# A decoder layer on one core: a short path for the last batch, filler matmuls at both ends, and one pair of rows issued by another engine

## The chip, the cores and the metric

The kernel runs on one NeuronCore of a Trainium2 chip. The core has a matrix engine (TensorE, PE in the profile, with its weight loads as PEld), a vector engine (VectorE, DVE), an activation engine (ScalarE, ACT), a general engine (GpSimd, POOL) and an engine that here only starts DMA transfers (SyncE, SP). Each engine runs its own list of instructions strictly in order; semaphores hold it back until what it needs is there. The metric is the device time of one execution in microseconds.

## The reference

32 sequences of 128 tokens by 512 features go through one decoder layer with LayerNorm after each of its three parts:

```python
x = _layernorm(x + _L0_attn_ref(x, Wq, Wk, Wv, Wo))          # causal, 16 heads of 32, rotary
x = _layernorm(x + _L0_xattn_ref(x, ctx, ctx, gamma))
x = _layernorm(x + _L0_ffn_ref(x, w1, b1, ln_g, ln_b, w2, b2))

def _L0_xattn_ref(q, k, v, gamma):       # q, k, v: (32, 128, 512), 8 heads
    qh = q.reshape(B, 8, 16, 512)        # the 512 features are the positions,
    kh = k.reshape(B, 8, 16, 512)        # 16 of the 128 tokens a head
    vh = v.reshape(B, 8, 16, 512)
    sm = softmax(einsum('bhdq,bhdl->bhql', qh, kh) / sqrt(16))
    return gamma * einsum('bhql,bhdl->bhdq', sm, vh).reshape(B, 128, 512)

def _L0_ffn_ref(x, ...):                 # 512 -> 2048 -> 512
    h = gelu(silu(bitlinear158(x, w1, b1)))
    h = layer_norm(h, ln_g, ln_b)
    return bitlinear158(h, w2, b2)       # x: RMS norm, 8-bit steps; w: -1, 0, 1
```

## The kernel before

**Two stages.** Stage one does the self-attention of all 32 batches, splits its result and the context into three bf16 parts, and writes them to HBM (`q_d`, `k_d`; six combinations of parts make one float32-like product). It also makes the FFN's weights ternary. Stage two takes each batch through the cross-attention and the FFN.

**An order written out ahead.** Both stages are lists of operations handed to `Plan` (L83). Each operation has an engine, an estimated cost, what it reads and writes, a priority (batch number plus an offset by kind from `OFF1` or `OFF2`) and sometimes an earliest time `rel`. `Plan.run` (L174) goes through them as a list scheduler: of the operations that could start within the same short interval (`slack`) it takes the one of lowest priority value, and emits its instructions. The result is one fixed order for each engine. The estimated times only make the order; on the chip an engine takes its next instruction when the semaphores let it.

**Start.** `split_weight` (L302) loads Wq and Wk together, Wv and Wo in sixteen tiles of 128x512 into four buffers `wst`. Each is split into a rounded part (`hi`, by ScalarE or VectorE, L315 and L317) and a remainder (`lo`, by VectorE, L318). `load` (L332) brings a batch's x in two forms. A projection (`project`, L346) is twelve matmuls of 128x128x512: hi by hi, lo of x by hi, hi by lo.

**From stage one to stage two.** `split3` (L350) ends a batch of stage one: ScalarE and GpSimd make the three parts, and SyncE issues six writes of them (L364). `early` (L578), run when the last projection is emitted, frees the projection weights' memory and loads K and Q parts of the first two batches of stage two there. In stage two, `b1_` forms for each half batch (four heads) sixteen blocks of scores (L677) of which VectorE takes the row maxima (L681). `shift` (L688) transposes these maxima on TensorE (L691), splits their negative into two bf16 rows (L694, L695), and SyncE copies both rows into the Q tile (L700), so that the second score matmul (`b2_`, L756) subtracts the maximum itself. ScalarE takes the exponential (L759). TensorE multiplies it (L766) with a tile `cT` of 32 columns a head: 16 of V, and 16 of ones, set by GpSimd at L616; so the sum of the weights stands in 16 equal rows beside the 16 result rows. `cT` is one of the tiles of stage two, and its memory held tiles of stage one.

**A batch's end in stage two.** ScalarE copies the result from PSUM to `f` (L773), SyncE writes it to HBM (`F`, L777). `final` (L834) reads back one row of sums a head as a 128x32 tile (`den`), takes the reciprocal (L841), writes it to HBM, reads it broadcast to 128x512 (`rden`), and reads the results as `num`; then num times rden (L846), plus x1 (L848), LayerNorm. `up_` (L896) makes 8-bit steps `q1`, transposes them by DMA (L914), and runs sixteen matmuls (L925) in four blocks, each taken out of PSUM by VectorE (L928). `gelu_` (L934) runs SiLU (L940) and GELU (L942) over the full 2048 columns on ScalarE, each with a table load. `down_` (L946) takes mean and variance (L952, L955), normalizes z (L794, L972 on GpSimd, L980, L991 on VectorE), takes its maximum and square sum (L998, L997), makes steps `q2`, transposes them by DMA (L1003), runs sixteen matmuls (L1009), adds (L1013), LayerNorm, and writes the output (L1016). For the last three batches (`last`) some steps go to VectorE instead of GpSimd and other PSUM banks are used.

The loop at the end of the stage, and the two lines by which shift's rows are copied:

```python
    for b in range(NB2):
        load(b)
        for g in range(2):
            b1_(b, g)
        for g in range(2):
            b2_(b, g)
        final(b)
        up_(b)
...
            for s, m in enumerate((hi, lo)):
                nc.sync.dma_start(q.t[NPR + s:NPR + s + 1].rearrange("p h (a c) -> p (h a) c", c=P), m.t)
```

Of the kernel before, what the change touches and what calls it, by code (L numbers as in the profile page):

```python
# [11 lines left out]
F32 = mybir.dt.float32  # L12
# [11 lines left out]
P = 128  # L24
# [40 lines left out]
CFG = dict(y0e='Pool', x2be='Pool', q2T=1, q1=2, tb2=3, boost=1.0, bank_mT='mx', bank_q1T='m', bank_z='m', bank_q2T='mx', bank_py='m', early=5, ssv=1, NQ=4, cT=3, f=2, num=1, x1=2, rden=2, x2=2, nb=32, mx=3, sT=3, acc=1, m=1, ex=8, mTe='DVE', acce='ACT', q1e='ACT', q2e='ACT', lne='Pool', ye='Pool', sce='Pool', mxw=1, stw=1, pair=1, z=3, xb=3, slack=0.05, last_lne='DVE', last_ye='DVE', last_sce='DVE', last_y0e='DVE', last_bank_mT='sT', last_bank_q1T='m', last_bank_z='sT', last_bank_q2T='mx', last_bank_py='sT', zm='PPPP', last_zm='FFFP', q1m='p', q2m='ad', last_q1m='d', last_q2m='ad')  # L65
OFF2 = {'SP.const': -264.67, 'x.kq': 390.3, 'SP.v': 77.29, 'PE.mx': -381.13, 'DVE.mx': 126.92, 'PE.mT': -632.22, 'DVE.mT': 8.23, 'SP.m': -156.28, 'PE.sT': -531.43, 'ACT.ex': -687.83, 'PE.pv': 37.38, 'ACT.acc': -737.17, 'SP.f': 49.63, 'SP.fd': 1119.71, 'SP.fn': 725.19, 'SP.fx': 343.0, 'DVE.rd': -172.57, 'SP.fr': -316.31, 'SP.fb': 17.98, 'Pool.y': -355.28, 'DVE.y': -82.99, 'Pool.yn': -277.59, 'DVE.c1': -57.25, 'Pool.c1': -358.01, 'Pool.c1m': -627.03, 'Pool.q1a': -78.8, 'Pool.x2b': 72.59, 'SP.q1T': -375.73, 'PE.c1': 39.79, 'DVE.z': -137.9, 'ACT.gelu': -406.78, 'DVE.nmu': -80.22, 'ACT.sq': -333.32, 'Pool.zn': -48.07, 'Pool.zt': 303.63, 'Pool.zb': -221.61, 'ACT.sq2': 252.58, 'DVE.am2': 91.79, 'Pool.c2': -682.87, 'Pool.c2m': -291.19, 'ACT.q2a': -262.61, 'DVE.q2a': -514.12, 'SP.q2T': 382.04, 'PE.c2': 86.97, 'DVE.c3': 17.23, 'Pool.c3': -278.83, 'Pool.c3n': 302.38, 'SP.out': 77.71, 'SP.kq': -42.69, 'DVE.yn': -735.62, 'DVE.c1m': 785.24, 'DVE.q1a': 467.22, 'DVE.zn': 550.15, 'DVE.zb': -508.13, 'DVE.c2m': -306.12, 'DVE.c3n': 99.96}
OFF1 = {'SP.x': 76.47, 'SP.w': -83.56, 'ACT.w': 1251.46, 'DVE.wl': 97.39, 'DVE.w': 1455.82, 'SP.wq': 258.11, 'ACT.wq': -501.07, 'DVE.wq': -718.11, 'PE.wq': 497.75, 'ACT.xh': -83.03, 'Pool.xl': -493.52, 'PE.qkv': 642.06, 'DVE.rope': -749.29, 'Pool.rope': 726.68, 'ACT.v': -277.88, 'SP.cx': 161.38, 'ACT.cs': 561.27, 'Pool.cs': 151.36, 'Pool.cs3': 444.12, 'SP.cs': -169.59, 'SP.ct': -341.75, 'ACT.ct': 5.76, 'SP.cv': 657.35, 'PE.qkT': -233.53, 'DVE.qkT': -713.26, 'PE.sc': 223.31, 'DVE.mask': -673.03, 'ACT.exp': 343.93, 'DVE.rd': 481.16, 'DVE.pr': 893.48, 'PE.prT': -342.18, 'DVE.prT': 602.51, 'ACT.prT': 121.56, 'Pool.pr': 38.32, 'PE.pv': 403.29, 'ACT.oh': 297.53, 'DVE.ol': -241.16, 'PE.wo': 645.28, 'DVE.y': -873.41, 'Pool.y': 255.11, 'Pool.x1': -113.85, 'SP.x1': 730.76, 'ACT.xs': 299.8, 'Pool.xs': -1039.81, 'Pool.xs3': 582.54, 'SP.xs': 975.4}
C1 = dict(pace=15.0, xs=4, pr=5, prT=7, ra=3, qkT=4, sp=3, spr=2, xhe='ACT', lne='Pool', s1e='Pool', s2e='ACT', cxl=-0.5, wq=3.0, nb=32, wst=4, mm=3, tr=3, sc=4, scc=1.1, po=1, pc=4, spe='ACT', cte='ACT', s3e='Pool', qke='DVE', pre=['DVE', 'DVE', 'Pool', 'Pool'], prTe=['DVE', 'ACT', 'ACT', 'ACT'], wl=24.0, slack=0.02)
# [152 lines left out]
def decoder_kernel(ctx: ExitStack, tc: tile.TileContext, x, xT, cx, cxT, wqkT, wvT, woT, gamma,  # L221
# [11 lines left out]
    make_identity(nc, ident)  # L233
    nhalf = const.tile([P, 1], F32, tag="nhalf", name="nhalf")
# [17 lines left out]
    k_d = [dram.tile([6, XD, XH, D], BF16, tag=f"kd{b}", name=f"kd{b}") for b in range(NB)]  # L252


    with ExitStack() as st1:
# [44 lines left out]


        def split_weight(name, wts, src, cols):  # L302
# [3 lines left out]
            for j in range(cols // 512):  # L306
                sl = slice(j * 512, (j + 1) * 512)
                w = pl.buf("w")
                halves.append(w)

                def part(c, sl=sl, w=w):
                    t = pl.buf("wst")
                    dma("w", lambda: nc.sync.dma_start(t.t, src[:, c, sl]), 262, (), (t,), -1.0)
                    if c % 2:
                        pl.op("DVE.w", 0.34, lambda: nc.vector.tensor_copy(hi[:, c, sl], t.t), (t,), (w,), -1.0)  # L315
                    else:
                        pl.op("ACT.w", 0.48, lambda: nc.scalar.copy(hi[:, c, sl], t.t), (t,), (w,), -1.0)  # L317
                    pl.op("DVE.wl", 0.6, lambda: nc.vector.tensor_tensor(  # L318
                        lo[:, c, sl], t.t, hi[:, c, sl].bitcast(F32), ALU.subtract), (t,), (w,), -1.0)
                for c in range(NC):  # L320
                    part(c)
            return hi, lo, halves

        def en(e):
            return nc.vector if e == "DVE" else nc.gpsimd
# [289 lines left out]
    for t in vring:  # L615
        nc.gpsimd.memset(t[:, XD:], 1.0)  # L616
# [468 lines left out]
```

## Time and profile before

| what | us |
|---|---|
| three runs | 1672.92, 1670.26, 1672.68 |
| their median | 1672.68 |
| the profiled execution, device time | 1675.28 |
| its span, first to last instruction | 1673.5 |
| first matmul of stage one (L346) | starts 10.29 |
| first score matmul of stage two (L677) | starts 563.48 |
| first copy of a result (L773) | 598.8 |
| last copy of a result (L773) | 1594.6 |
| mean granted clock of TensorE, share of full speed | 0.973 |

A profiled execution gives one row for an instruction, or for a run of equal ones: start, duration, engine, line of the code, operation, destination and source, count, and in brackets how long the engine stood idle before it and what ended that wait. `SPq` marks the time SyncE spends on issuing a DMA. "Busy" for TensorE includes the time a matmul spends in the pipeline, so equal matmuls in a row are better priced by the distance of their starts. The granted clock says which share of full speed the throttle let TensorE have in a stretch.

### The profile page before, as it was taken

The numbers are of one execution on the slowest core, as the hardware profiler recorded it, in microseconds if no ns is written. First come the engines' busy times: TensorE is split into PE (matmuls) and PEld (weight loads), VectorE is DVE, ScalarE is ACT, GpSimd is POOL, SyncE is SP. The second block draws the span as 40 slices with busy tenths as digits, with TensorE's granted clock in tenths as the row PEclk, the third lists the DMA queues.
The fourth block names the chain that finished last, engine by engine and source line by source line (L and its number), as shares of the span: only waits on it lengthen the run. The fifth ranks groups of instructions, "written<-read, shape, count | busy, mean of one in ns | idle before, by whom it ended". The sixth has DMA issues, their size and how long they took to land.

```text
span 1673.5 us, 30270 instructions
## 1 busy us (share of the span) xinstructions
PE 1551.4 (93%) x9540; PEld 785.0 (47%) x9540; DVE 1383.9 (83%) x3315; ACT 1432.7 (86%) x2950; POOL 1251.5 (75%) x1679
## 2 busy tenths in 40 slices
PE   6999999999999799999999999999999999999844
PEld 4878777777778333333333333333333333333211
DVE  6877776777777678899999989899899999998674
ACT  4889989899976367999989989899999999998963
POOL 3777778777787404679879888878978888986772
PEclk8999999999999799999999999999999999999977
DMA  6476677766664654355455345545544544544221
GB/s 226 163 236 232 226 231 244 255 233 214 209 208 153 185 177 122 93 129 145 113 133 147 105 129 139 131 115 139 142 110 128 153 110 134 149 122 123 69 62 50
DMA packets 235680, 258.71 MB, mean 155 GB/s; under 512 B 110072, under 2 KB 159224, under 8 KB 235136
## 3 DMA queue, kind: packets, MB, share of 16 engines
q1 hardware_dynamic: 235520, 256.78, 52.8%
q8 instruction: 75, 1.23, 0.3%
q14 instruction: 85, 0.70, 0.1%
HBM read 142.41 MB, written 92.81 MB: 141 GB/s over the span
## 4 chain that ended last, share of the span: by engine, by line
PE 41%; DVE 18%; POOL 16%; DMA 9%; ACT 8%; issue 7%; SPq 1%; POOLq 0%; ACTq 0%; DVEq 0%
PE banka L346 12%; DVE mt L681 8%; PE acc L766 7%; PE sT L756 6%; POOL z L972 6%; PE mx L677 5%; PE m L925 2%; DVE am L998 2%; PE banka L477 2%; DMA qd<-sp 2%; POOL z L794 2%; PE banka L447 2%; ACT pr L465 1%; ACT ex L759 1%; PE banka L496 1%
## 5 line engine op out<-in xcount | busy, mean ns | idle before, releaser
L681 DVE TENSOR_REDUCE mt<-mx 128x1 f32<-128x512 f32 x1024 | 643.4, 679 | 54.9 <-PE mx L677 52.9
L759 ACT ACTIVATE ex<-sT 128x512 f32<-128x512 f32 x1024 | 533.9, 615 | 77.9 <-PE sT L756 74.4
L677 PE MATMUL mx<-kp,qp 96*128 96x512 bf16 x1024 | 336.9, 386 | 21.5 <-DVE mt L681 17.7
L756 PE MATMUL sT<-qp,kp 98*128 98x512 bf16 x1024 | 320.7, 385 | 15.9 <-DMA qp<-mlo 13.3
L766 PE MATMUL acc<-ex,cT 128*32 128x512 f32 x2048 | 289.4, 637 | 0.0
L465 ACT ACTIVATE pr<-pr,nm 128x128 f32<-128x128 f32 x512 | 198.9, 394 | 4.1 <-DVE nm L459 4.1
L756 PEld LDWEIGHTS <-kp 98*128 98x128 bf16 x1024 | 90.3, 98 | 223.7 <-issue 125.1
L677 PEld LDWEIGHTS <-qp 96*128 96x128 bf16 x1024 | 96.3, 98 | 195.5 <-issue 95.1
L972 POOL TENSOR_TENSOR z<-z,bb_b 128x512 f32<-128x512 f32 x119 | 154.4, 1301 | 0.3
L972 POOL TENSOR_TENSOR z<-z,g_b 128x512 f32<-128x512 f32 x119 | 153.5, 1297 | 0.5
L459 DVE CUSTOM_DVE_ANT_0 pr<-banka,cmask 128x128 f32<-128x128 f32 x512 | 111.0, 286 | 35.9 <-PE banka L447 35.2
L1009 PE MATMUL m<-w2q,q2T 128*128 128x512 fp8e4 x464 | 116.7, 385 | 16.4 <-DMA q2T<-q 16.4
L766 PEld LDWEIGHTS acc<-ex,cT 128*32 128x32 f32 x2048 | 70.6, 184 | 114.1 <-issue 108.8
L925 PE MATMUL m<-w1q,q1T 128*128 128x512 fp8e4 x464 | 119.1, 378 | 2.7 <-DVE z L928 1.3
L1009 PEld LDWEIGHTS <-q2T 128*128 128x128 f16 x512 | 51.0, 101 | 104.5 <-DMA q2T<-q 34.9
L465 ACT ACTIVATION_READ_ACCUMULATOR pr<-pr,nm 128x1 f32 x512 | 98.0, 191 | 0.0
L794 POOL TENSOR_SCALAR z<-z,nmu,rs 128x512 f32<-128x512 f32 x119 | 94.5, 801 | 1.8
L361 POOL TENSOR_TENSOR sp<-spr,sp 128x512 bf16<-128x512 f32 x64 | 76.7, 1200 | 20.3 <-ACT sp L359 18.2
L928 DVE SCALAR_TENSOR_TENSOR z<-m,dq,b_b 128x512 f32<-128x512 f32 x116 | 85.0, 733 | 1.8 <-PE m L925 1.5
L925 PEld LDWEIGHTS <-q1T 128*128 128x128 f16 x512 | 49.2, 97 | 76.1 <-issue 19.9
L846 POOL TENSOR_TENSOR num<-num,rden 128x512 f32<-128x512 f32 x29 | 37.1, 1278 | 62.3 <-DMA rden<-rd 62.2
L346 PE MATMUL banka<-wqkh,xh 128*128 128x512 f32 x256 | 73.9, 411 | 10.3 <-ACT xh L388 10.3
(152 smaller groups left out, 3247.9 us busy)
## 6 DMA issues: line engine op xcount, KB each, us to landing
kd<-sp SPq DMA_DIRECT2D x192, 128.0 KB
qd<-sp SPq DMA_DIRECT2D x192, 128.0 KB
kp<-kd SPq DMA_DIRECT2D x64, 384.0 KB
qp<-qd SPq DMA_DIRECT2D x64, 384.0 KB
F<-f SPq DMA_DIRECT2D x64, 256.0 KB
xt<-in_xT SPq DMA_DIRECT2D x32, 256.0 KB
xs<-in_x SPq DMA_DIRECT2D x32, 256.0 KB
ct<-in_cxT SPq DMA_DIRECT2D x32, 256.0 KB
```

The costliest lines, as they stand in the source:

```text
L346: nc.tensor.matmul(pq.t, parts[a].t[:, c, :], w[t][:, c, sl], start=k == 0, stop=k == 11)
L459: nc.vector.tensor_tensor_reduce(pr.t[:, c, :], sc.t[:, c * P:(c + 1) * P], cmask, -1.0, 3e38, ALU.add, ALU.min, nm.t[:, c:c + 1])
L465: nc.scalar.activation(pr.t[:, c, :], pr.t[:, c, :], AF.Exp, scale=-1.0, bias=nm.t[:, c:c + 1], accum_out=den.t[:, c:c + 1])
L677: nc.tensor.matmul(sc.t[:, j, :], q.t[0:NPR, h, (qc + j) * P:(qc + j + 1) * P], k.t[0:NPR, h, :], start=True, stop=True)
L681: pl.op("DVE.mx", 0.064 + 0.534 * W, lambda: nc.vector.tensor_reduce(mt.t[:, i:i + W], sc.t, AX.X, ALU.max), (sc,), (mt,), p, join=True)
L756: nc.tensor.matmul(sc.t[:, i, :], k.t[:, h, lc * P:(lc + 1) * P], q.t[:, h, :], start=True, stop=True)
L759: pl.op("ACT.ex", 0.052 + 0.426 * SW, lambda: nc.scalar.activation(ex.t[:, j:j + SW, :], sc.t, AF.Exp, scale=1.0 / XD ** 0.5), (sc,), (ex, ...
L766: nc.tensor.matmul(acc.t[32 * h:32 * h + 32, :], v.t[:, :, XH * lc + 4 * g + h], exs[h // 2].t[:, h % 2, :], start=lc == 0, stop=lc == NC - 1)
L794: pl.op(e + "." + p, cost + 0.1, lambda: en(e).tensor_scalar(o.t[:, sl], v.t[:, sl], sh.t, sc.t, ALU.add, ALU.mult), ins, outs, prio)
L925: nc.tensor.matmul(flat(pz)[:, i * 512:(i + 1) * 512], q1T.t[:, c, :], w1q[:, c, (n + i) * 512:(n + i + 1) * 512], start=c == 0, stop=c == ...
L972: pl.op(e + kind, 0.148 + 0.0021 * w if e == "Pool" else 0.05 + 0.00105 * w, lambda: en(e).tensor_tensor(t(), t(), other[:, sl], op), src, ...
L1009: nc.tensor.matmul(flat(py)[:, 0:D], q2T.t[:, c, :], w2q[:, c, :], start=c == 0, stop=c == NI - 1)
```

## The change

1. **Start.** The sixteen weight tiles are staged in sixteen tiles (seven `prT`, five `pr`, four `wst`), not four. GpSimd takes six of the sixteen remainders. The first batch's x has the first priority. 28 matmuls of constants, 128x128 by 512 columns, are entered into the plan at 0.6 to 7.35 us.
2. **Between the stages.** The six writes of parts are issued by ScalarE for the last three batches of stage one. `cT` moves to the memory that the projection weights leave. The first half batch's two shift rows are issued by ScalarE.
3. **Last batch** (`quick`). `f` goes by DMA inside SBUF to `num` and `rden`, with no HBM between, issued by ScalarE and SyncE; the reciprocal is taken of the 128x512 tile `rden`. `q1` and `q2` are transposed on TensorE (with an fp16 identity) and copied from PSUM. SiLU and GELU run in quarters of 512 columns; mean and variance of z come from VectorE's statistics instruction.
4. **Fillers in stage two.** One at its start; and 500 matmuls of constants, 128x128 by 256 columns, entered at 985 to 1050 us of the plan's time, the first of them after the last result copy, with the weakest priority.
5. **Numbers.** All offsets `OFF1` and `OFF2` are new; `slack` of stage one is 0.05, not 0.02; a projection matmul is planned at 0.244, not 0.236; `slow` is 1.0 for all batches.

```diff
-CFG = dict(y0e='Pool', ...
+CFG = dict(fill0=0.2, fill1=(985.0, 1050.0), qk=1, y0e='Pool', ...
-C1 = dict(pace=15.0, ...
+C1 = dict(fill=7.0, late=3, pace=15.0, ...
...
+    fillw = const.tile([P, D], BF16, tag="fillw", name="fillw")
+    nc.vector.memset(fillw, 0.5)
+
+    def fill(tag, times, after=(), cols=256):
+        v = pl.buf(tag)
+
+        def one(t, ins):
+            pl.op("PE.fill", 0.22 * cols / D, lambda: nc.tensor.matmul(
+                v.t[:, 0:cols], fillw[:, 0:P], fillw[:, 0:cols], start=True, stop=True), ins, (v,), 1e6, rel=t)
+        for i, t in enumerate(times):
+            one(t, after if i == 0 else ())
...
+        stage = ["prT"] * C1["prT"] + ["pr"] * C1["pr"] + ["wst"] * C1["wst"]
...
-                    t = pl.buf("wst")
-                    dma("w", lambda: nc.sync.dma_start(t.t, src[:, c, sl]), 262, (), (t,), -1.0)
+                    tag = stage.pop(0)
+                    t = pl.buf(tag)
...
+                    dma("w", lambda: nc.sync.dma_start(flat_(), src[:, c, sl]), 262, (), (t,), -1.0)
...
-                    pl.op("DVE.wl", 0.6, lambda: nc.vector.tensor_tensor(
-                        lo[:, c, sl], t.t, hi[:, c, sl].bitcast(F32), ALU.subtract), (t,), (w,), -1.0)
+                    e = "Pool" if c == 3 or c == 1 and name != "wqk" else "DVE"
+                    pl.op(e + ".wl", 0.6 if e == "DVE" else 1.23, lambda: en(e).tensor_tensor(
+                        lo[:, c, sl], flat_(), hi[:, c, sl].bitcast(F32), ALU.subtract), (t,), (w,), -1.0)
...
-            dma("x", lambda: nc.sync.dma_start(xt.t, xT[b]), 262, (), (xt,), at, (b - 1.5) * C1["pace"])
+            dma("x", lambda: nc.sync.dma_start(xt.t, xT[b]), 262, (), (xt,), at if b else -1000.0, (b - 1.5) * C1["pace"])
...
-                dma(kind, lambda s=s, k=k: nc.sync.dma_start(dst[s].rearrange("t h c -> h t c"), sp.t[:, k, :]), 131,
-                    (sp,), (), prio)
+                q = nc.scalar if late else nc.sync
+                pl.op("ACT.xsd" if late else "SP." + kind, 0.55, lambda s=s, k=k, q=q: q.dma_start(
+                    dst[s].rearrange("t h c -> h t c"), sp.t[:, k, :]), (sp,), (), prio, 2.6)
...
-            split3("xs", x1, q_d[b], Q_PARTS, at)
+            split3("xs", x1, q_d[b], Q_PARTS, at, b >= NB1 - C1['late'])
...
+        fill("po", [0.6 + 0.25 * i for i in range(int(C1['fill'] / 0.25))], cols=512)
...
+            for i in range(CFG["cT"]):
+                t = qk.tile([P, 2 * XD, NC * XH], F32, tag=f"cT{i}", name=f"cT{i}")
+                nc.gpsimd.memset(t[:, XD:], 1.0)
+                vring.append(t)
...
-                nc.sync.dma_start(q.t[NPR + s:NPR + s + 1].rearrange("p h (a c) -> p (h a) c", c=P), m.t)
-        pl.op("SP.m", 1.0, fn, (hi, lo), (q,), at, 2.2)
+                (nc.scalar if at == 0.5 else nc.sync).dma_start(
+                    q.t[NPR + s:NPR + s + 1].rearrange("p h (a c) -> p (h a) c", c=P), m.t)
+        pl.op("ACT.m" if at == 0.5 else "SP.m", 1.0, fn, (hi, lo), (q,), at, 2.2)
...
+        if b == NB2 - 1 and g == 1:
+            LASTF.append(f)
+        if quick(b):
+
+            if g == 0:
+                F[b] = pl.buf("num"), pl.buf("rden")
+
+            def place(q, o, r):
+                for h in range(4):
+                    n = XD * (4 * g + h)
+                    q.dma_start(o.t[n:n + XD], f.t[32 * h + r:32 * h + r + XD])
+            num, rden = F[b]
+            pl.op("SP.qf", 1.8, lambda: place(nc.sync, rden, XD), (f,), (rden,), at, 2.6)
+            pl.op("ACT.qf", 0.5, lambda: place(nc.scalar, num, 0), (f,), (num,), at, 4.0)
+            return
...
+            pl.op("DVE.qrd", 0.7, lambda: nc.vector.reciprocal(rden.t, rden.t), (rden,), (rden,), at)
...
+    def turned(p, o, v, n, e, pt, at):
+
+        def view():
+            return flat(pt).bitcast(FP16)[:, 0:512]
+
+        def turn():
+            for c in range(NC):
+                nc.tensor.transpose(view()[:, c * P:(c + 1) * P], v.t[:, n * 512 + c * P:n * 512 + (c + 1) * P], ident16)
+        pl.op("PE." + p, 0.6, turn, (v,), (pt,), at)
+        pl.op(f"{e}.{p}", 0.5 if e == "ACT" else 0.6, lambda: cp(e)(
+            o.t[:, NC * n:NC * n + NC, :].rearrange("p a b -> p (a b)"), view()), (pt,), (o,), at, join=n > 0)
...
+            def quarter(n):
+                sl = slice(512 * n, 512 * n + 512)
+                pl.op("ACT.qg", 0.62 if n else 1.9, lambda: nc.scalar.activation(z.t[:, sl], z.t[:, sl], AF.Gelu), (z, zs), (z, zs), at)
+                pl.op("DVE.qs", 0.62, lambda: nc.vector.bn_stats(st.t[:, 6 * n:6 * n + 6], z.t[:, sl]), (z,), (st,), at, join=n > 0)
...
+    fill("m", [0.13 * i for i in range(int(CFG['fill0'] / 0.13))])
+    lo, hi = CFG['fill1']
+    fill("acc", [lo + 0.13 * i for i in range(int((hi - lo) / 0.13))], LASTF)
```

## The prediction

> **What bounds the kernel now.** I read the page first, then busy time by stretch, then the order of time at three places: the start, the change from stage one to stage two, and the end.
>
> ```profile
> span 1673.5 us, 30270 instructions
> PE 1551.4 (93%) x9540; PEld 785.0 (47%) x9540; DVE 1383.9 (83%) x3315; ACT 1432.7 (86%) x2950; POOL 1251.5 (75%) x1679
> ...
> PEclk8999999999999799999999999999999999999977
> ```
>
> TensorE is the fullest engine. In the stretches it stands at 50.00 of 50 us (50 to 100), 99.02 of 100 (100 to 200), and 193 to 197 of 200 in stage two, where VectorE and ScalarE have 184 to 189 as well. So the middle has little to give. The weak places are three:
>
> ```profile
> 0.00:10.00 10.00, 0.00 (x0) 0.00 (x0) 3.43 (x6) 2.90 (x4) 1.17 (x13) 1.00 0.70 232
> 20.00:30.00 10.00, 7.36 (x23) 5.63 (x22) 8.44 (x14) 2.37 (x4) 4.44 (x4) 0.67 0.49 147
> ...
> 580.00:590.00 10.00, 4.45 (x11) 1.46 (x11) 2.03 (x4) 3.07 (x6) 1.45 (x3) 0.51 0.28 81
> ...
> 1610.00:1620.00 10.00, 0.00 (x0) 0.00 (x0) 9.84 (x12) 5.16 (x6) 8.70 (x15) 0.50 0.36 79
> 1650.00:1660.00 10.00, 0.00 (x0) 0.00 (x0) 6.68 (x10) 3.15 (x3) 4.17 (x7) 0.73 0.11 21
> ```
>
> After the stretch come busy time of PE, PEld, DVE, ACT and POOL, then granted clock, DMA share and GB/s. In these places TensorE is idle and its granted clock falls to 0.5 to 0.7.
>
> **The start.** TensorE begins at 10.29 us and first runs without gaps from 32.24. Until then it is busy 6.65 + 4.54 + 5.06 = 16.25 us, idle 16.0. Its 40 projection matmuls (L346) took 15.3 us there; four in a row took 1.91 us, later 0.94 (0.235 each), so 40 are worth 9.4 and 5.9 us went to the low clock. The loss is 21.9 us. What holds it: sixteen weight tiles come through four buffers, each waiting for its split. With sixteen buffers, and x first (issued at 3.53 now, about 1.2 then), the loads set the pace: x and the twelve tiles of Q, K and V are 13 x 0.262 = 3.4 MB, at 232 to 257 GB/s (the first two ten-us stretches) 13 to 15 us; with issue, landing, the last split and its last eight matmuls that is 20 to 21 us instead of 32.24. This is at most 12 us. At least 2 are x's earlier issue. VectorE must still split most tiles (0.69 us for a low part); GpSimd takes six of the sixteen at 1.27 to 1.34 us (row L389, the same kind), hidden by its idle time (5.8 of 20 us busy to 20). The 28 fillers of 512 columns cost 0.217 us warm and 0.425 cold: 8 cold and 20 warm make 7.7 us, from about 1.5 to 9.2, so they may hold the first real matmul for a microsecond. I take **-8**, nearer to the load bound, as the splits then overlap it.
>
> **Between the stages.**
>
> ```profile
> 574.43 4.06 PE L677 MATMUL mx<-kp,qp 96*128 96x512 bf16 x7 [0.21 <-DVE mt L681]
> 574.59 0.28 DVE L695 SCALAR_TENSOR_TENSOR mlo<-mx,mhi 16x128 bf16<-16x128 f32 x1
> ...
> 582.37 0.33 SPq L663 DMA_DIRECT2D cT<-cd  x1
> 582.75 0.62 SPq L700 DMA_DIRECT2D qp<-mhi  x1
> 583.42 0.57 SPq L700 DMA_DIRECT2D qp<-mlo  x1
> ...
> 585.55 1.44 PE L756 MATMUL sT<-qp,kp 98*128 98x512 bf16 x3 [7.06 <-DMA qp<-mlo]
> ```
>
> The shift's two rows are ready at 574.87 and are issued at 582.75: SyncE first stands before cT's load, whose memory the last qd write (landed 582.23) still holds. TensorE waits 7.06 us and then runs 11 matmuls at 0.425 instead of 0.217 us, 2.3 more: 9.4 in all. Moved to ScalarE, the rows queue behind six qd writes that ScalarE now issues for the last batch, after GpSimd's third part (573.39). An issue is 0.33 to 0.65 us on SyncE: those end at 575.4 to 577.3, the two rows at 576.1 to 578.6, and 2.1 us to landing (583.42 to 585.52) gives 578.2 to 580.7, against TensorE's last matmul at 578.49. So 7 to 9.4 us go; if the rows land as slowly as x1d's writes in this crowd (5.4 us), 4 to 6. ScalarE's 18 issues (6 to 12 us) hide in its idle time: 13.05 of 20 us busy at 540 to 560, 2.77 of 20 at 560 to 580. Past SyncE, cT's load is no longer late either (its memory comes from the projection weights). I take **-8**.
>
> The Trainium skill (DMA: Bandwidth & Descriptors, Issuing engines are not separate DMA queues) says that DMAs of all issuers share the same 16 engines and that a second issuer saves only issue time, usually little. By it this part would be worth about the two issues, 1.2 us. The rows above say otherwise, as the wait was in the queue.
>
> **The end**, first the last batch's chain. Its last f copy starts at 1594.59, 78.9 us before the end.
>
> ```profile
> 1594.59 0.59 ACT L773 COPY f<-acc 128x512 f32<-128x512 f32 x1 [3.96 <-PE acc L766]
> 1602.54 0.34 DVE L841 RECIPROCAL den<-den 128x32 f32<-128x32 f32 x1
> 1611.24 1.75 DVE L846 TENSOR_TENSOR num<-num,rden 128x512 f32<-128x512 f32 x1
> 1622.36 1.19 SPq L914 DMA_TRANSPOSE q1T<-q  x1
> 1657.80 1.93 SPq L1003 DMA_TRANSPOSE q2T<-q  x1
> 1662.14 4.99 PE L1009 MATMUL sT<-w2q,q2T 128*128 128x512 fp8e4 x16 [12.66 <-DMA q2T<-q]
> ```
>
> - The way of f through HBM, four transfers with a reciprocal between, ends at about 1609.5 (14.3 us after 1595.2). Instead: four issues of 0.33 to 0.6 us (SyncE and ScalarE side by side), 2.1 to 4.5 to landing (den<-F: 1597.96 to 1602.5): 4 to 6 us. But the reciprocal is now of 128x512. The rows: 128x4 takes 0.169 us, 128x32 0.347, so 6.3 ns an element and 512 take 3.4; bounds 0.68 (other 128x512 rows) and 5.6 (16 x 0.347). Gain 5.6. ScalarE's four issues a half batch, 1.3 to 2.6 us, stand ahead of the Silu of the batch before, which then starts later by that much; SyncE's stand ahead of that batch's outputs and transposes, and it waits more than it issues there.
> - q1T by DMA: 1622.36 to the matmul at 1625.65, 3.3 us; four transposes (0.6) and a copy (0.68) 1.4: gain 1.9.
> - Silu by quarters: the last needs about 0.6 after the last z, not 1.91: gain 1.3. GELU by quarters with the statistics on VectorE: from 1639.80 to GpSimd's 1645.30 is 5.5 us; four quarters at 0.6, 0.69, 0.18, 0.15 and gaps are 3.7: gain 1.8.
> - q2T: 1657.80 to 1662.14, then 4.99 cold; transposes and copies in turn 2.7, then 16 x 0.217 = 3.5: gain 3.1. Warm clock in the matmuls of the chain before it (1633.10 and 1634.76): 1.0 + 1.4.
>
> Together -16; the batches before it share VectorE (50 of these 79 us busy), which gets 3.4 + 2 + 2.8 + 0.3 = 8 us more, so I call the chain alone **-15**, between -22 and -5.
>
> The Trainium skill (VectorE: DVE Perf Modes, First, the fixed hardware budget) has the reciprocal as an iterative divide repeated 8 times; at 0.96 GHz (Trainium Kernel Development and Optimization, NeuronCore Architecture) that makes 4.3 us an estimate for 512 elements. The sum would be 0.9 us longer.
>
> **The fillers of the end** speak against this. int(65 / 0.13) = 500 matmuls of 256 columns come after the last f copy, in order, on TensorE, whose program must end too. At half of 0.217 each they are 54 us warm (108 cold). After 1594.46 TensorE has 112 real matmuls, 24.2 us warm; with 20 small transposes (about 2 us) the sum is 80 us if the same work is left, 70 with the FFN of only the last two batches, 63 with that of only the last. TensorE's waits for late results come on top, as fillers behind a waiting matmul can't run. I take 75, the middle of 70 and 80, for the 78.9 of now: **-4**, bounds -16 and +8. If so, filler matmuls are the last thing to run and the shortened chain is hidden behind them.
>
> **The rest.** Constants, one filler at stage two's start, and the new priorities, which deal the fixed order anew: no row prices this. I take 0; TensorE's idle time bounds it: 9.2 us at 200 to 500 could be gained, and 15 lost.
>
> **Sum:** 1675.3 (the profiled execution's own time: span 1673.5 and 1.8 around it) - 8 - 8 - 4 = **1655**. The runs' median, 1672.68, lies 2.6 below that execution. Runs of this kernel spread by 0.16%, so under 0.2% is no change: 1669.3 to 1676.0.
>
> **Rivals.**
> - *The chain decides, not the fillers* (28%): little real work is left after the last f copy, or their planned places fit. For it: 47 us of TensorE idle in the last 79; against: 54 + 24 us. 1675.3 - 8 - 8 - 15 = 1644, 1634 to 1649.
> - *The head start is lost in the middle* (16%): DMA shares of 0.72 at 100 to 300 and waits there say that loads, not TensorE, could decide; against: 99% busy. 1675.3 - 8 - 4 = 1663, to 1674.
> - *Slower: the new fixed order leaves TensorE waiting in every batch of stage two* (14%). Place: the score matmuls L677, which already wait 16.0 us for the maxima of VectorE at 600 to 1540. A batch takes 31.6 us (f copies: 598.8 to 1594.6, 63 halves) for 29.6 of matmul time. It decides from 20 / 31 = 0.65 us a batch; with 1 us, 1655 + 31 = 1686. Against: VectorE's 92% leaves room to recover.
> - *The clock isn't held*: if matmuls of constants don't raise it, the fillers take up to 108 us and this is the slower side too; I count it there.
>
> **Numbers.** My forecast has 42%, its own range 1648 to 1664. Range 1636 to 1673: it leaves out some of the best chain and most of the slower case. Faster: 41 + 28 + 12 = 81%; no change: 1 + 3 + 2 = 6%; slower: 1 + 12 = 13%.
>
> **What would show it.** Start: no gaps on TensorE from about 20 to 24 us. Change of stages: no 7 us wait at L756, rows issued by ScalarE. Reciprocal of 128x512 at 3.4 us. End: whether TensorE's last instruction is a filler, after the last output's LayerNorm, and the distance from the last f copy to the end, 75 us. I am wrong if that distance is near 60, or if the f copies come further apart than 15.8 us.

## The result and the profile after

The changed kernel is slower: 1682.27 us, median of 5 runs (1678.29 to 1688.33), against 1672.68 in 5 runs of the kernel before beside them (1668.52 to 1676.16). The ratio is 1.0072, with a 95% interval of 1.0055 to 1.0090. The prediction, 1655 with a range of 1636 to 1673, was wrong in sign. The profiled execution took 1684.42 us, 9.1 more than the one before, and the landmarks of both say where:

| stretch (us, profiled executions) | before | after | difference | predicted |
|---|---|---|---|---|
| start to first score matmul of stage two (L677, now L703) | 563.48 | 562.17 | -1.3 | -8 |
| from there to the first result copy (L773, now L804) | 35.34 | 41.39 | +6.0 | -8 |
| 63 half batches, first to last result copy | 995.77 | 988.67 | -7.1 | 0 |
| last result copy to the end | 78.9 | 90.4 | +11.5 | -4 |

So in these two profiles the middle became faster, where nothing was expected, and both ends of stage two slower, where the gain was expected. How much of each landmark is chance is said with the experiments. The page of the changed kernel, its head, TensorE's clock and the group of the first score matmuls:

```profile
span 1682.6 us, 31392 instructions
PE 1611.2 (96%) x10089; PEld 833.8 (50%) x10089; DVE 1393.4 (83%) x3319; ACT 1431.1 (85%) x2955; POOL 1256.5 (75%) x1685
...
PEclk9999999999999799999999999999999999999999
...
L703 PE MATMUL mx<-kp,qp 96*128 96x512 bf16 x1024 | 336.5, 386 | 19.3 <-DVE mt L707 15.7
```

The fillers hold the clock to the end (9s where before two 7s stood) but for one stretch: at 1622 to 1632 us, where TensorE stands 3.90 us, it is 0.66. TensorE is 60 us busier. A score matmul waits for VectorE as little as before.

The start and the two weak places, in the view of busy time by stretch (after the stretch: PE, PEld, DVE, ACT, POOL, then granted clock, DMA share, GB/s):

```profile
0.00:10.00 10.00, 8.56 (x29) 3.61 (x30) 3.40 (x7) 3.75 (x5) 3.13 (x15) 1.00 0.73 221
10.00:20.00 10.00, 6.44 (x26) 4.33 (x26) 9.97 (x15) 4.59 (x7) 6.38 (x6) 0.99 1.05 385
20.00:30.00 10.00, 10.00 (x40) 8.10 (x39) 5.89 (x10) 4.20 (x7) 9.03 (x8) 0.84 0.68 237
...
580.00:590.00 10.00, 1.61 (x4) 0.59 (x5) 0.00 (x0) 1.11 (x4) 1.15 (x1) 0.50 0.48 152
1610.00:1620.00 10.00, 10.00 (x82) 7.83 (x81) 9.25 (x11) 4.56 (x5) 9.06 (x13) 1.00 0.29 54
```

The start did what was said of it: TensorE's last gap there ends at 19.67 us (before at 27.18). Between the stages it stands still longer than before (busy 1.61 of 10 us, before 4.45). At 1610 it is full, but most of it are fillers. The change of stages, in order of time:

```profile
565.78 7.37 SPq L388 DMA_DIRECT2D qd<-sp  x6
...
572.99 0.27 DVE L720 TENSOR_SCALAR mhi<-mx 16x128 bf16<-16x128 f32 x1
...
573.25 0.89 SPq L545 DMA_DIRECT2D x1d<-x  x2
...
573.29 0.28 DVE L721 SCALAR_TENSOR_TENSOR mlo<-mx,mhi 16x128 bf16<-16x128 f32 x1
...
576.82 0.77 POOL L543 TENSOR_SCALAR x<-ya,nm,rs 128x512 f32<-128x512 f32 x1 [10.96 <-DMA x1d<-x]
...
577.62 0.62 ACT L377 CAST sp<-x 128x512 bf16<-128x512 f32 x1 [14.79 <-POOL x L543]
...
579.52 5.06 ACTq L388 DMA_DIRECT2D qd<-sp  x7
...
584.68 0.61 ACTq L726 DMA_DIRECT2D qp<-mhi  x1
585.39 0.61 ACTq L726 DMA_DIRECT2D qp<-mlo  x1
...
588.39 1.01 PE L787 MATMUL sT<-qp,kp 98*128 98x512 bf16 x2 [11.19 <-DMA qp<-mlo]
```

The rows are ready at 573.57 and go out at 584.68, now behind ScalarE's qd writes and, ahead of these, its cast, which stands 14.79 us for GpSimd, which stands 10.96 us for a write of x1d. TensorE waits 11.19 us where it waited 7.06. `x1d` is the copy of x1 that SyncE writes to HBM for stage two; a later x1 takes the same memory, so GpSimd can't write it before that copy has been read out. The chain of waits shows how that got so late:

```profile
564.17 7.16 DMA qd<-sp
571.35 0.57 SPq L388
...
573.25 3.40 DMA x1d<-x
...
576.82 0.77 POOL x L543
```

SyncE's queue stands at 565.78 to 573.15 in six qd writes of an earlier batch, and the transfer it waits for is a qd write that ScalarE issued. The built program says why: every DMA of SyncE and of ScalarE is given one of eight completion semaphores, mostly in turn, and waits for the DMA that had it before, whichever engine issued that. So SyncE, which the writes were to relieve, stands for their ends all the same.

The last result copy and what ScalarE does before it, in its own order of time:

```profile
1587.85 2.46 ACTq L815 DMA_DIRECT2D num<-f  x4
1590.36 0.60 ACT L790 ACTIVATE ex<-sT 128x512 f32<-128x512 f32 x1 [3.64 <-DMA num<-f]
1592.23 0.58 ACT L804 COPY f<-acc 128x512 f32<-128x512 f32 x1 [1.27 <-PE acc L797]
```

VectorE behind it:

```profile
1598.03 3.34 DVE L887 RECIPROCAL rden<-rden 128x512 f32<-128x512 f32 x1
...
1604.74 0.68 DVE L903 TENSOR_TENSOR num<-num,rden 128x512 f32<-128x512 f32 x1
...
1609.36 0.69 DVE L905 TENSOR_TENSOR num<-num,x 128x512 f32<-128x512 f32 x1
...
1621.32 0.48 DVE L948 TENSOR_SCALAR q<-x,c 128x512 f16<-128x512 f32 x1
...
1648.01 0.75 DVE L1111 SCALAR_TENSOR_TENSOR x2b<-sT,dq,x2b 128x512 f32<-128x512 f32 x1 [2.68 <-PE sT L1107]
...
1654.25 2.27 DVE L1092 TENSOR_REDUCE am<-z 128x1 f32<-128x2048 f32 x1
```

And TensorE at the end:

```profile
1637.69 6.82 PE L264 MATMUL acc<-fillw 128*128 128x256 bf16 x61
1644.35 3.62 PE L1107 MATMUL sT<-w2q,q2T 128*128 128x512 fp8e4 x16
1647.80 10.53 PE L264 MATMUL acc<-fillw 128*128 128x256 bf16 x95
...
1661.15 3.62 PE L1107 MATMUL sT<-w2q,q2T 128*128 128x512 fp8e4 x16
1664.60 17.19 PE L264 MATMUL acc<-fillw 128*128 128x256 bf16 x156
```

The last real matmuls take 3.62 us, 4.99 before. But the product of results and reciprocals, ready sooner, is followed 4.6 us later by the sum with x1, with other batches' steps between, and the last batch's q1 comes 29.1 us after the last result copy (before 27.3), its maximum (`am`) 62.0 us after it (before 57.8). Then 156 fillers remain and end the program, 13.8 us after the last LayerNorm step (which ends at 1668.0).

### The profile page after: what moved, and what is told of

Its sections match the earlier page's. It is cut to its first block, busy times and chain, and to the rows that moved or that the text cites. A ratio compares the mean times of both kernels' runs of the same rounds, so it can differ in the third digit from the quotient of the medians.

```text
span 1682.6 us, 31392 instructions
## 1 busy us (share of the span) xinstructions
PE 1611.2 (96%) x10089; PEld 833.8 (50%) x10089; DVE 1393.4 (83%) x3319; ACT 1431.1 (85%) x2955; POOL 1256.5 (75%) x1685
## 4 chain that ended last, share of the span: by engine, by line
PE 40%; POOL 17%; DVE 16%; DMA 11%; ACT 9%; issue 4%; SPq 2%; ACTq 0%; POOLq 0%; DVEq 0%
PE banka L369 9%; PE acc L797 7%; DVE mt L707 7%; PE sT L787 6%; POOL z L1066 6%; PE mx L703 6%; PE m L997 2%; DVE am L1092 2%; DMA wst<-in_w2T 2%; PE banka L501 2%; PE acc L264 2%; ACT ex L790 2%; POOL z L840 2%; ACT pr L489 1%; PE m L1107 1%
## 5 line engine op out<-in xcount | busy, mean ns | idle before, releaser
L790 ACT ACTIVATE ex<-sT 128x512 f32<-128x512 f32 x1024 | 534.2, 617 | 72.7 <-PE sT L787 65.2
L703 PE MATMUL mx<-kp,qp 96*128 96x512 bf16 x1024 | 336.5, 386 | 19.3 <-DVE mt L707 15.7
L787 PE MATMUL sT<-qp,kp 98*128 98x512 bf16 x1024 | 321.8, 385 | 17.5 <-DMA qp<-mlo 13.8
L703 PEld LDWEIGHTS <-qp 96*128 96x128 bf16 x1024 | 96.1, 98 | 198.0 <-issue 96.9
L501 PE MATMUL banka<-ident,pr 128*128 128x128 f32 x512 | 76.2, 275 | 9.0 <-POOL pr L494 4.3
```

Source lines behind the costliest of these rows:

```text
L703: nc.tensor.matmul(sc.t[:, j, :], q.t[0:NPR, h, (qc + j) * P:(qc + j + 1) * P], k.t[0:NPR, h, :], start=True, stop=True)
L787: nc.tensor.matmul(sc.t[:, i, :], k.t[:, h, lc * P:(lc + 1) * P], q.t[:, h, :], start=True, stop=True)
L790: pl.op("ACT.ex", 0.052 + 0.426 * SW, lambda: nc.scalar.activation(ex.t[:, j:j + SW, :], sc.t, AF.Exp, scale=1.0 / XD ** 0.5), (sc,), (ex, ...
```

## The experiments

Ratios are to runs of the kernel before on the same chip, with 95% intervals. They are not the quotient of the two medians in the row, and differ from it by up to 0.15%. A time is the median of the runs. "f" is the last result copy.

| kernel | us | before | ratio | interval |
|---|---|---|---|---|
| 344 fillers, not 500 | 1673.15 | 1672.45 | 1.0019 | 1.0003 to 1.0034 |
| no fillers at the end | 1674.67 | 1672.45 | 1.0013 | 1.0001 to 1.0025 |
| 344, rows and writes by SyncE | 1666.81 | 1672.45 | 0.9965 | 0.9950 to 0.9981 |
| 344, writes by SyncE, rows by ScalarE | 1667.54 | 1672.45 | 0.9972 | 0.9958 to 0.9987 |
| SyncE, stage one's old order | 1670.34 | 1676.80 | 0.9961 | 0.9944 to 0.9978 |
| SyncE, old start | 1673.43 | 1676.80 | 0.9988 | 0.9971 to 1.0005 |
| SyncE, result rows by SyncE too, 305 | 1667.15 | 1676.80 | 0.9944 | 0.9926 to 0.9961 |
| SyncE, short path for two batches, 330 | 1666.93 | 1676.80 | 0.9944 | 0.9925 to 0.9963 |
| both of these two, 344 | 1667.57 | 1672.39 | 0.9975 | 0.9960 to 0.9991 |
| both, no fillers at the end | 1669.86 | 1672.39 | 0.9987 | 0.9973 to 1.0001 |
| SyncE, no fillers at the end | 1669.88 | 1672.39 | 0.9986 | 0.9972 to 1.0000 |
| the same without the short path | 1662.57 | 1672.39 | 0.9944 | 0.9927 to 0.9962 |
| the same, later half of the short path | 1662.07 | 1672.78 | 0.9939 | 0.9922 to 0.9956 |
| the same, first half of the short path | 1662.75 | 1672.78 | 0.9938 | 0.9919 to 0.9956 |
| the same, whole, result rows by SyncE | 1667.06 | 1672.78 | 0.9962 | 0.9948 to 0.9977 |

How much of a landmark is chance: ten of these kernels have the same order of stage one on every engine, and the first score matmul of stage two comes in their profiles at 559.23 to 568.88 us. So a difference of several us in this landmark between two profiles may be chance. Two distances vary less. From this matmul to the first result copy, those ten and the kernel with rows by ScalarE alone take 32.2 to 34.2 us. From f to the end, five kernels with the same order at the end and the same 344 fillers take 77.9 to 79.0 us. The edits at the end leave the order of everything before the last batches as it was.

### The fillers behind the last matmul

```diff
-CFG = dict(fill0=0.2, fill1=(985.0, 1050.0), qk=1, ...
+CFG = dict(fill0=0.2, fill1=(985.0, 1029.8), qk=1, ...
```

> The changed kernel without its last 156 filler matmuls; every other instruction of every engine stands in the same order. Theory A (the fillers behind the last real matmul end the program): TensorE's last filler at 1681.8 us goes, the last output lands some 3 us after the last LayerNorm step (1668.0), so the time falls by about 11 us, from 1682.3 to 1671, level with the kernel before. Rival B (the fillers' end hides nothing, the output transfers end the program anyway): within 3 us of 1682.

The second kernel has `fill1=(985.0, 985.0)`, no filler at the end at all.

> The changed kernel without any of the 500 fillers at the end (one filler at stage two's start and the 28 at the beginning stay). Theory A (the fillers' clock is worth little, as TensorE is not what the end waits for): 1669 to 1673, the same as with 344 fillers. Rival B (the warm clock pays as forecast, 1.0 + 1.4 + 1.5 us on the chain): 3 to 4 us slower than with 344 fillers, about 1675, with the last 16 down matmuls at about 5.0 us, not 3.6.

The first is 0.53% under the change (1.0019 / 1.0072), 9 us, with every other instruction in the same order: the 156 fillers behind the last matmul cost that. Without any fillers the time is not clearly another (medians 1673.15 and 1674.67, ratios 1.0019 and 1.0013). The last down matmuls with 344 fillers, and TensorE's end without any:

```profile
1661.37 3.62 PE L1107 MATMUL sT<-w2q,q2T 128*128 128x512 fp8e4 x16
```

```profile
1628.69 6.36 PE L997 MATMUL sT<-w1q,q1T 128*128 128x512 fp8e4 x16 [1.56 <-DVE q1T L962]
1634.89 3.62 PE L1107 MATMUL sT<-w2q,q2T 128*128 128x512 fp8e4 x16
...
1662.39 4.91 PE L1107 MATMUL sT<-w2q,q2T 128*128 128x512 fp8e4 x16
```

Without fillers the last matmuls are cold again (4.91 us, granted clock 0.74, for 3.62 at 1.00). Four pairs of kernels differ in the end's fillers and, but for a few VectorE steps in the last pair, in nothing else:

| pair | f to the end with fillers | without | ratios |
|---|---|---|---|
| the change's order | 78.2 | 81.1 | 1.0019, 1.0013 |
| SyncE | 78.2 | 80.9 | 0.9965, 0.9986 |
| SyncE, result rows by SyncE too | 74.5 | 78.3 | 0.9944, 0.9962 |
| SyncE, result rows too, two batches | 72.7 | 78.2 | 0.9975, 0.9987 |

In the profiles, fillers that end before the last real matmul shorten the end by 2.7 to 5.5 us, about what the clock was forecast to bring (3 to 4). In the times three pairs lean the same way by 0.1 to 0.2% and one doesn't, each within overlapping intervals, so the times alone don't settle it.

### The rows and the writes between the stages

```diff
-C1 = dict(fill=7.0, late=3, ...
+C1 = dict(fill=7.0, late=0, ...
...
-                (nc.scalar if at == 0.5 else nc.sync).dma_start(
+                nc.sync.dma_start(
...
-        pl.op("ACT.m" if at == 0.5 else "SP.m", 1.0, fn, (hi, lo), (q,), at, 2.2)
+        pl.op("SP.m", 1.0, fn, (hi, lo), (q,), at, 2.2)
```

> 344 fillers, and the middle undone: the six writes of all batches and the first shift's rows are issued by SyncE as before (cT stays in the weights' memory). Theory A (moving the writes and rows to ScalarE made the wait at the second score matmul longer, 11.2 us for 7.1): the wait is 6 to 8 us and the time is 3 to 5 us below that of 344 fillers alone. Rival B (the wait comes from GpSimd's late third part, whoever issues): the wait stays at 10 to 12 us, same time.

The fourth kernel has only `late=0`, so ScalarE issues the two rows alone.

> 344 fillers; the first shift's rows are issued by ScalarE, but the six writes of the last three batches go back to SyncE. Theory A (the rows stand behind the writes in ScalarE's queue): with nothing ahead of them the rows go out at about 573.6 and land at 576 to 579; the wait at the second score matmul falls from 11.2 to under 2 us and the time is 8 to 11 us below that of 344 fillers alone, about 1661. Rival B (an issue waits for an earlier transfer of the other queue, since both draw on the same eight completion semaphores): the rows go out only when SyncE's writes have landed, and the wait stays above 6 us.

With everything on SyncE the time falls by another 0.54% (0.9965 / 1.0019), 9 us (6.3 by the medians); the profiles show 5.5 at the first result copy (601.92 to 596.41) and 6.8 at the last. From the first score matmul to the first result copy the three kernels with 18 writes on ScalarE take 39.2 to 41.4 us, where the thirteen without take 27.9 to 34.2. SyncE's rows in this kernel, in order of time:

```profile
575.32 0.28 DVE L721 SCALAR_TENSOR_TENSOR mlo<-mx,mhi 16x128 bf16<-16x128 f32 x1
...
577.30 0.40 SPq L689 DMA_DIRECT2D cT<-cd  x1
578.03 0.61 SPq L726 DMA_DIRECT2D qp<-mhi  x1
578.74 0.55 SPq L726 DMA_DIRECT2D qp<-mlo  x1
...
583.20 1.01 PE L787 MATMUL sT<-qp,kp 98*128 98x512 bf16 x2 [3.97 <-DMA qp<-mlo]
```

The wait is 3.97 us, before the change 7.06: cT's load no longer stands, as its memory is free. That this part of the change is good is read from the trace; it was not tried by itself. With the rows alone on ScalarE, in the view by order of time:

```profile
571.65 0.60 ACTq L726 DMA_DIRECT2D qp<-mhi  x1
571.65 0.28 DVE L721 SCALAR_TENSOR_TENSOR mlo<-mx,mhi 16x128 bf16<-16x128 f32 x1
...
575.07 0.53 ACTq L726 DMA_DIRECT2D qp<-mlo  x1
577.80 1.44 PE L787 MATMUL sT<-qp,kp 98*128 98x512 bf16 x3 [2.24 <-DMA qp<-mlo]
...
580.65 3.21 ACT L790 ACTIVATE ex<-sT 128x512 f32<-128x512 f32 x6 [7.74 <-DMA qd<-sp]
```

They go out 6.4 and 3.7 us earlier, but in this profile the rows are also ready 3.7 us earlier. Counted from its own maximum, the second row goes out no sooner: 3.14 us after it is ready in both kernels, here because it has the first row's semaphore and waits for its landing. TensorE starts 5.4 us earlier, three matmuls fill their banks, and the wait moves on: the exponential stands 7.74 us for a qd write. In the built program it waits for all eight semaphores, and so for those writes too. The time is the same (intervals 0.9950 to 0.9981 and 0.9958 to 0.9987). So what costs in the change is the 18 writes on ScalarE. That the end of the writes is the bound behind the rows is read from this trace.

### The start and stage one's order

```diff
-        stage = ["prT"] * C1["prT"] + ["pr"] * C1["pr"] + ["wst"] * C1["wst"]
+        stage = ["wst"] * 16
...
-                    e = "Pool" if c == 3 or c == 1 and name != "wqk" else "DVE"
+                    e = "DVE"
```

This with no fillers at the start and the first batch's x at its old priority undoes the start. The other kernel has the old `OFF1`, `slack` and planned matmul cost. Both are made from the kernel with SyncE's rows.

> The kernel with 344 fillers and SyncE's rows and writes (median 1666.8), but stage one in the order that the old numbers make (old offsets, old slack, a projection planned at 0.236); the new start stays. Theory A (the new order of stage one spends the head start of some 6 us between 50 and 400 us): 2 to 5 us faster, about 1663, and the first score matmul of stage two at about 560. Rival B (the loads and the other engines spend it, whatever the order): within 1.5 us of 1666.8.

> The same kernel with the start undone: four staging tiles, no fillers at the start, remainders on VectorE, x without the first place; the new order numbers stay. Theory A (the new start is worth its 6 us of matmul work): 4 to 8 us slower, about 1673. Rival B (the middle of stage one spends any head start): within 2 us of 1666.8.

The start is worth 0.9988 against 0.9965, 0.23% or 4 us; the two intervals overlap slightly, so it may be less. Of the old start, by stretch:

```profile
0.00:10.00 10.00, 0.00 (x0) 0.00 (x0) 3.19 (x7) 2.52 (x3) 1.17 (x13) 1.00 0.68 219
10.00:20.00 10.00, 6.25 (x16) 4.67 (x16) 6.74 (x11) 5.23 (x8) 6.34 (x7) 0.98 0.84 254
20.00:30.00 10.00, 6.95 (x22) 5.46 (x23) 9.30 (x15) 1.24 (x2) 2.62 (x3) 0.67 0.69 205
```

The gaps are back, up to 27.13 us, and 76 projection matmuls are done by 50 us, not 116. Forty are 9.4 us at 0.235 each, and yet the end moves by some 4. In the change the lead over the kernel before was 35 projection matmuls at 50 us (116 to 81), 25 at 100, 10 at 200 and 4 at 400. Stage one's old order gives the same time as the new (0.9961 and 0.9965), so the new order didn't eat the lead. In the profile its first score matmul came at 570.46 us, not at the 560 expected, 6.3 us after the new order's; at the first result copy (598.35) 1.9 us of that were left. What ate the lead, the loads or the split writes, was not tried.

### The short path of the last batch

First two attempts to save it: the result rows of `num` issued by SyncE instead of ScalarE, and the short path for two batches (`qk=2`), each with the trailing fillers cut; then both together, with and without fillers.

```diff
-            pl.op("ACT.qf", 0.5, lambda: place(nc.scalar, num, 0), (f,), (num,), at, 4.0)
+            pl.op("SP.qf", 1.8, lambda: place(nc.sync, num, 0), (f,), (num,), at, 4.0)
```

> The same kernel, but all eight copies of the last batch's result rows are issued by SyncE, none by ScalarE; 305 fillers, as many as stand ahead of the last real matmul in this order. Theory A (ScalarE stands 3.6 us behind its four issues in the middle of the last attention): the last result copy comes 2 to 4 us earlier and the time is 2 to 3 us lower, about 1664. Rival B (the later rows cost it again, or the earlier batches set the end): within 1 us of 1666.8.

> The same kernel with the short path for the last two batches, not one (330 fillers, none behind the last real matmul). Theory A (the end is a chain of transfers and waits, the short path cuts it): another 3 to 8 us faster, about 1661. Rival B (VectorE's and GpSimd's work on the batches before fills the end, and the short path adds 8 us of VectorE's time a batch): no gain or 1 to 6 us slower, 1667 to 1673.

> The short path for the last two batches and all their result rows issued by SyncE, with 344 fillers, none behind the last real matmul. If the two single gains (each about 0.2% against SyncE's rows alone) add: ratio to the kernel before about 0.992. If both cured the same wait: 0.994 to 0.995.

> The same as the kernel before it in this list without the 344 fillers. If the warm clock of the end is worth its forecast 3 to 4 us: 3 to 4 us slower than with them. If fillers in front of real matmuls cost about what the clock brings: within 2 us.

Each alone lies 0.2% under the kernel they come from, within the intervals; together they lie above it, which neither expectation had. In the profiles the end is shorter with all three: f to the end is 74.5, 74.8 and, for both, 72.7 us, where the kernel they come from has 78.2. The times don't settle whether that is a gain. ScalarE's exponential no longer stands for the row copies (0.38 us, not 3.64), but the last result copy then waits 3.93 us for TensorE. It comes 12.9 us after the copy before it, 13.5 where ScalarE issues, so the 2 to 4 us expected are not there.

Then the path itself, without fillers in the way: with it, without it (`qk=0`), and the two halves. The first half is the result kept in SBUF with the large reciprocal (L807, L883), the later half is quarters, statistics and transposes on TensorE (L983 to L1097).

```diff
-        if quick(b):
+        if False and quick(b):
```

> SyncE's rows and writes, the short path for the last batch, no fillers at the end. To be read against the next kernel, which lacks the short path. Theory A (the short path's gain is lost to the batches before it on VectorE and GpSimd): from the last result copy to the end 78 to 81 us, as before the change (78.9); time within 2 us of the next kernel's. Rival B (the short path does cut the end and other edits hid it): 5 us or more below the next kernel.

> The same with the long path for the last batch too (result through HBM, transposes by DMA, whole SiLU and GELU). Theory A: 78 to 82 us from the last result copy to the end, time within 2 us of the kernel with the short path. Rival B: 84 us or more, time 5 us or more above it.

> As the kernel with the short path and no end fillers (ratio 0.9986 to before), but the last batch's result goes through HBM again with the small reciprocal; only the later half of the short path stays (SiLU and GELU in quarters, statistics on VectorE, both transposes on TensorE). Theory H, the first half costs (ScalarE's issues stall the exponential by 3.6 us and the reciprocal takes 3.3 us of a full VectorE): ratio near that without the short path, 0.994 to 0.996, and no stall of the exponential on num. Theory T, the later half costs (its copies and statistics on VectorE): it stays at 0.998 to 1.000.

> The other half alone: the last batch's result stays in SBUF with the reciprocal of 128x512, and the rest of the batch goes the long way. Theory H: it keeps the cost, 0.998 to 1.000. Theory T: 0.994 to 0.996. If both halves lie near 0.996, the cost is shared or is lost in how each order is dealt anew.

> The whole short path without end fillers, but all copies of the result's rows issued by SyncE, none by ScalarE. If the stall of ScalarE is the price: 0.994 to 0.996. If it is the work of VectorE: 0.998 to 1.000, with the exponential's idle time gone all the same.

As it stands in the change the path costs: 0.9986 with it, 0.9944 without, intervals apart, 7 us, of which the two profiles show 3.4. Either half alone costs and gains nothing (0.9939, 0.9938), which neither theory had. Result rows by SyncE lie between (0.9962). So no form of the path without fillers is faster than the long path. From the last f to the last batch's maximum `am`, and to the end, in the profiles:

| kernel, none with end fillers | f | f to `am` | f to the end |
|---|---|---|---|
| long path | 1583.56 | 55.9 | 77.5 |
| first half | 1580.75 | 55.4 | 76.9 |
| later half | 1581.19 | 58.4 | 77.6 |
| whole | 1583.61 | 63.3 | 80.9 |
| whole, rows by SyncE | 1586.14 | 59.9 | 78.3 |

Behind `am` the whole path is 4.0 us shorter than the long one (17.6 for 21.6), as it was meant to be; ahead of it 7.4 us are lost. VectorE's `am` with the long path, and VectorE of the kernel with the whole path:

```profile
1639.43 2.29 DVE L1092 TENSOR_REDUCE am<-z 128x1 f32<-128x2048 f32 x1
```

```profile
1635.98 0.75 DVE L1074 SCALAR_TENSOR_TENSOR z<-z,nmu,g_b 128x512 f32<-128x512 f32 x1
1640.63 0.75 DVE L1111 SCALAR_TENSOR_TENSOR x2b<-sT,dq,x2b 128x512 f32<-128x512 f32 x1 [3.89 <-PE sT L1107]
...
1642.77 1.38 DVE L1074 SCALAR_TENSOR_TENSOR z<-z,nmu,g_b 128x512 f32<-128x512 f32 x2
...
1646.87 2.27 DVE L1092 TENSOR_REDUCE am<-z 128x1 f32<-128x2048 f32 x1
```

The last batch's statistics are there early, its first quarter is normalized at 1635.98, and then VectorE stands 3.89 us for batch 30's down matmuls, whose sum is next in the written order, before it takes the last batch's other quarters. The change has the same wait at 1648.01, 2.68 us. VectorE is also 6.2 us busier from 1580 us on (59.2 against 53.0 without the path; the last f copies lie at the same time, 1583.6). That these two things make the whole path worse than its halves is read from the trace and was not tried by itself.

Five kernels lie lowest, at 0.9938 to 0.9944, clearly faster than both kernels, and all have SyncE's rows and writes: the long path or either half without end fillers, and the whole path with its result rows by SyncE, or for two batches, with fillers. Which of them is best isn't shown, and the long path with fillers was not run.

## Why the prediction was wrong

- **Between the stages, -8, was +6.0** in the two profiles. The step that failed is "those end at 575.4 to 577.3, the two rows at 576.1 to 578.6". It gave ScalarE's queue the issue times and GpSimd's finish of the profile before. But the writes by ScalarE delayed SyncE's through the shared semaphores, SyncE's x1d write delayed GpSimd's last split (a wait of 10.96 us, before 2.81), and the rows went out at 584.68. I had named the queue behind which the rows stand, and not asked what the moved writes wait for and who waits for those. That SyncE's cT load held up the rows was right: moved, the wait is 3.97 us with SyncE issuing all. But its memory was not that of the qd writes: in the built program of the kernel before it held tiles of x1 and of the sum ahead of it (`ya`), and the load waited for counts on all eight semaphores, those writes among them. The Trainium skill (DMA: Bandwidth & Descriptors, Issuing engines are not separate DMA queues) says that a second issuer saves only issue time, usually little; the two runs agree: with the rows alone on ScalarE no time was saved (0.9972, and 0.9965 with all on SyncE).
- **The end, -4, was +11.5.** The mechanism was right, that fillers are the last thing to run; the size wasn't. I took 75 us from the last f copy, between 70 and 80; it was 90.4. TensorE was busy 83.0 of it, 57.6 in fillers (I had 54) and 25.5 in real matmuls: all the work of the 80 case was left, so leaning to 70 had no ground. And 7.4 us TensorE stood idle, mostly in waits of real matmuls that no filler could use, which I named and gave no price. With 90.4 in place of 75 alone the sum would have been 1670.
- **The chain alone, -15, gave no gain that the runs show**: without fillers f to the end is 80.9 with the path, 78.3 with its result rows by SyncE, and 77.5 without the path. That is the larger error, hidden behind the fillers. The step that failed is the sum "Together -16" with only 1 us taken off for VectorE. The single steps were priced well: the reciprocal took 3.34 us (3.4 taken; the estimate of 4.3 worked out from the Trainium skill, VectorE: DVE Perf Modes, First, the fixed hardware budget, was too much), num times rden came 4.1 us sooner after f (5.6 taken), the last down matmuls took 3.62. But I added up savings of one batch's chain in a stretch in which VectorE works on three batches in a fixed order. I counted 8 us more for VectorE (the terms make 8.5) and charged 1; it was 6.2 busier, and `am` came 7.4 later. That VectorE's written order is what eats the gain is read from the trace; with either half alone nothing is lost, so the cause stays open in part.
- **The start, -8, is some 4 at the end of the program**, and the intervals overlap, so it may be none. TensorE's gaps closed as said; the rival that the head start is lost in the middle was half right: the lead in matmuls was gone by 400 us. Two readings there were off. TensorE's last gap before the change ends at 27.18 us, not 32.24; from there it ran without gaps at a granted clock of 0.50. And the granted clock doesn't show what slowed the first matmuls: at 10 to 16 us it is 1.00, where four took 1.91 us.
- **The new order, 0, was -7.1** in the two profiles: half batches 15.69 us apart, not 15.81. The same stretch is 986.8 to 992.9 us in all 13 profiles with this order and at most one batch on the short path, and 995.8 in the only profile of the kernel before; so a gain is likely, and its size isn't shown. The slower rival, a wait per batch in stage two, was wrong; the page's wait for `mt` is 15.7 us (before 17.7). So was "the clock isn't held": the granted clock is 1.00 at 1610 to 1620 us, and the 156 last fillers took 0.110 each. The kernel became slower by a way that no rival had, both ends of stage two together. The sum also started from the profiled execution, 2.6 us above the median of the runs.

## What to carry over

Filler matmuls must end before the last real one: count them against the idle time that is there, and measure what the clock they hold buys, with and without them in the same order. Shortening one batch's chain need not save anything where an engine that it shares with other batches works through a written order; look at what stands before each of its steps in that order. Where a whole program's time varies by more than the edit is worth, compare the distance between two landmarks on either side of the edit. Before a transfer is moved to another engine's queue, find out what that transfer waits for, which semaphore it shares, and who waits for its end.

## What the runs showed of the hardware

- The reciprocal on VectorE costs by the element: 3.34 us for 128x512, where 128x32 took 0.34 before, a slope of 6.2 ns for each element of a row; a product of the same shape takes 0.68.
- In this case matmuls of a constant 0.5 in bf16 held the granted clock: 1.00 at 1610 to 1620 us, where 61 such fillers of 256 columns a little later took 6.82 us, 0.112 each; before, TensorE idle, it was 0.50 there.
- Issuing isn't free for a computing engine: seven writes kept ScalarE's queue 5.06 us, and four row copies 2.46 us; the exponential behind those stood 3.64 us, and 0.38 where SyncE issued them.
